# One core of Trainium2, an attention block of 2048 tokens: the order of GpSimd's instructions in the last block of queries

## The chip, the cores and the metric

The kernel runs on one core of a Trainium2 chip. The core has five engines that run their own instruction streams and meet through semaphores: TensorE (PE in the profile), VectorE (DVE), ScalarE (ACT), GpSimd (POOL) and SyncE (SP, which here only issues DMAs). DMAs are issued by SP, ACT and POOL; an issuing instruction stands in the queue of its engine like any other. The metric is the device time of one execution in microseconds. Before the change it is 1636.91 us, the median of 3 runs (1634.71 to 1638.35).

## The reference: what is computed

One layer over x of shape (1, 2048, 512): multi-head latent attention, a residual and a layer norm, then a linear layer with scale and bias, a residual and a second layer norm.

```python
cq = rms_norm(x @ w_qa.T, q_a_ln_w)              # 384 wide
q = (cq @ w_qb.T).reshape(b, s, H, 192)          # 16 heads: 128 "nope" and 64 rotary
ckv = x @ w_kva.T                                # 128 latent and 64 rotary
k_nope, v = split(rms_norm(ckv[..., :128], kv_a_ln_w) @ w_kvb.T)
scores = q_full @ k_full.T * 192 ** -0.5         # causal
out = softmax(scores) @ v                        # fp32 softmax
x = layernorm(x + out.reshape(b, s, 2048) @ w_o.T)
x = layernorm(x + x @ (weight * scale_weight[:, None]).T + bias)
```

The kernel works on latents: the key weights are folded into the queries, and the value and output weights into one product per head (wvo), so that the attention itself reads only the 128-wide latent and the rotary part.

## The kernel before, in words

**Blocks, pairs, units, heads.** The queries are cut into 4 blocks b of 512, the 16 heads into 8 pairs p, a block into 4 tiles qt of 128 queries. `units` (line 698) runs for each block over the pairs, the tiles, and (outside block 0) the two heads j of the pair. I call (b, p, qt) a unit and one head of it a half step; k = 2 qt + j counts the eight half steps of a pair. In block 3 a unit has 1664 to 2048 keys, in two tiles of up to 1024.

**A half step of block 3**, in the code's order (lines 750 to 763):

1. `settle` (line 461), where j is 0: for the units whose sums are complete, DVE adds them, takes the reciprocal and turns it (L468 to L473), and POOL writes the result to a small DRAM tensor, `rows` (16 KB, L476).
2. `prepare_output` (line 865): loads for the output, at fixed half steps, issued by POOL. In pair 6: `wv` at k = 2 (1 MB, L871). In pair 7: the first part of `wo` at k = 1 (1 MB, L862), `o` and `iv` of pairs 0 and 1 of block 0 at k = 2 and 3 (512 KB each, L823 and L839), the second part of `wo` at k = 4, `o` of pair 2 at k = 7. At k = 5 and 6 DVE and ACT multiply and split what pairs 0 and 1 brought (`latent_split`, L849, L64, L65).
3. `head_scores` (line 483): PE writes the scores into PSUM (L438, L441); DVE takes the maximum (L510) and the bias (L517, L518). In between the head before runs on: ACT copies its probabilities to fp16 (L563), POOL subtracts to get the low part (L564, two instructions), DVE transposes both (L546) and SP sends them to `ring` in the layout that the values need (L553). Then ACT takes the exponentials (L532), into `pr` tiles of which there are five.
4. `fill`: parts of the projection of the next pair, or in pair 7 of `value_output` (L198, which reads `wv` and `wo`).
5. `run_values` (line 795): half a unit of values. The first half of `values` (line 603) has POOL load `iv`, the reciprocals of the sums, from `rows` into all partitions (128 KB, L612, two buffers); PE multiplies the first keys (L619). The second half does the other keys, and DVE multiplies the result with `iv` into `ot` (L628), which SP writes to DRAM. In the steady state the first half of unit u stands in the second half step of the unit two later, and the second half in the first half step of the unit three later.

**After the last unit** (lines 930 to 957) PE accumulates the output of pairs 0 and 1 of block 0 (`accumulate`, L888). After the second accumulation of pair 0 the code finishes the last head, calls `settle`, and asks POOL for `o` of pair 3 (L823) and `iv` of pairs 2 and 3 (L839), and SP for the other two parts of `wo`. `latent_split` of pair 2 follows, then the last values, then `latent_split` of pair 3. What comes later in the code reads the rest of `o` and `iv` through SP.

**What sets the order.** The framework's planner runs a timeline of its own when the kernel is built, and from it picks the order of instructions of each engine. Inside `tc.manual_schedule(engines=...)` the engines named keep the order of the code. From block 1 on PE and SP are named (line 914). From the unit (3, 0, 1) on, DVE and ACT are named too (line 729), until the end of the last values (the ExitStack `ctx_f`). POOL is ordered by the planner throughout. So `rows`, `iv`, the loads of `prepare_output` and the subtractions L564 stand on POOL where the planner put them: the trace shows `rows` of a unit behind the two L564 of its last head, `iv` of a unit from about the time at which one of its two buffers is free, and four of the loads of pair 7 at 1280 us, while the scores of pair 6 are running.

Of the kernel before, what the change touches and what calls it, by code (L numbers as in the profile page):

```python
# [49 lines left out]
def mla_block(ctx: ExitStack, tc: tile.TileContext, a, out):  # L50
    nc = tc.nc
    ET = mybir.EngineType
# [140 lines left out]
    def value_output(p, pool, tag):  # L193

        wvo = state["wvo"][p]
        for j in range(2):
            ps = pool.tile([P, HID], F32, tag=tag, name=f"ps_wo{2 * p + j}")
            nc.tensor.matmul(ps, state["wv"][:, 2 * p + j], state["wo"][2 * p + j], start=True, stop=True)  # L198
            split(ps, wvo[:, 0, j, :], wvo[:, 1, j, :], kvln_o)
            yield  # L200
# [125 lines left out]
    def put_in(all=False):  # L326
        kept = []
        for n, dst, src in later:
            if n == 0 or all:
                nc.sync.dma_start(dst, src)  # L330
            else:
                kept.append([n - 1, dst, src])
        later[:] = kept
# [65 lines left out]
    def project_nope(b, p, direct=None):  # L399
        if direct is None and ("wq", b, p) not in state:  # L400
            load_wq(b, p)
        w = state.pop(("wq", b, p)) if direct is None else direct
        cq = state["cq"]
        qn = blk.tile([P, 2, 2, QB], F32R, tag="qn", name=f"qn{b}_{p}")
        for j in range(2):
            ps = psum["m"].tile([P, QB], F32, tag="m", name=f"ps_qn{b}_{p}_{j}")
            n = 0
            for lt in range(LT):
                for i, k in ((0, 0), (0, 1), (1, 0)):
                    nc.tensor.matmul(  # L410
                        ps, w[:, i, lt, j * P : (j + 1) * P], cq[:, k, lt, :], start=n == 0, stop=n == 8
                    )
                    n += 1
            split(ps, qn[:, 0, j, :], qn[:, 1, j, :], kvln)
            if j == 1:
                state["qn", b, p] = qn
                if b or p == NPAIR - 1:
                    load_wq(*((b, p + 1) if p + 1 < NPAIR else (b + 1, 0)))
                if p == NPAIR - 1:
                    load_block(b + 1)  # L420
            yield

    def project(b, p):
        if p % 2 == 0:
            yield from project_pe(b, p // 2)
        yield from project_nope(b, p)
# [144 lines left out]
    def pair_scores(pool, b, p, qt, nk):  # L571
        t = 4 * b + qt
        r = rq[:, t : t + 1]
        w = max(nk, 256)
        ps = psum["s"].tile([P, 2, 512], F32, tag="s", name=f"s{b}_{p}_{qt}")
        for mask in [score(ps[:, j, :], 0, w, b, p, j, qt, nk - P) for j in range(2)]:
            mask()
        neg = small.tile([P, 2], F32, tag="neg", name="neg")
        nc.vector.tensor_reduce(neg, ps[:, :, :nk], axis=AX.X, op=ALU.max, negate=True)
        bias = small.tile([P, 2], F32, tag="bias", name="bias")  # L580
        nc.vector.tensor_scalar(bias, neg, r, LOG_UP, ALU.mult, ALU.add)
        pr = pool.tile([P, 2, nk], F32, tag=f"pr{qt}", name=f"pr{b}_{p}_{qt}")
        for j in range(2):
            nc.scalar.activation(
                pr[:, j, :],
                ps[:, j, :nk],
                AF.Exp,
                bias=bias[:, j : j + 1],
                scale=r,
                accum_out=sums_of(b, p, qt, j),  # L590
            )
        return pr
# [41 lines left out]
    def fill(n=1):  # L634
        while n > 0 and fillers:
            try:
                next(fillers[0])
                n -= 1
            except StopIteration:
                fillers.pop(0)  # L640

    def drain():
        while fillers:
            fill()
# [48 lines left out]
    def flush():  # L693
        while probs:
            for _ in probs.pop():
                pass

    def units(pool, ring, b):
        lag = min(ring.shape[1] // (2048 * (b + 1)) - 1, 3) if b else 2

        for p in range(NPAIR):
            put_in(True)


            if p + 1 == NPAIR:
                at = (1, 2, 4, 5) if b < NB - 1 else (1, 3, 5, 7)
            elif p % 2 == 0 and p + 2 < NPAIR:
                at = (0, 1, 2, 3) if (b, p) == (1, 0) else (0, 1, 3, 4)
            else:
                at = (3, 4)  # L710
            if b and p % 2 == 0 and p + 2 < NPAIR:
                fillers.append(project_pe(b, p // 2 + 1))
            if p + 1 < NPAIR:
                fillers.append(project(b, p + 1) if b == 0 else project_nope(b, p + 1))
            elif b + 1 < NB:
                fillers.append(project(b + 1, 0))
            if b == NB - 1 and p == NPAIR - 1:
                ctx_p.close()
                pcr = state["pcr"] = ctx.enter_context(
                    tc.tile_pool(name="pcr", bufs=2, side="right", reuse_waits="tile")  # L720
                )
                state["wvo"] = [pcr.tile([P, 2, 2, HID], F32R, name=f"wvo{p}", bufs=1) for p in range(EARLY)]
                for i in range(EARLY):
                    fillers.append(value_output(i, psum["m"], "m"))
                at = (3, 4, 5, 6)
            for qt in range(4):
                nk = (4 * b + qt + 1) * P
                if (b, p, qt) == (NB - 1, 0, 1):
                    ctx_f.enter_context(tc.manual_schedule(engines={ET.PE, ET.SP, ET.DVE, ET.Activation}))
                if (b, p, qt) == (0, NPAIR - 1, 3):  # L730
                    s0, PT = -4 * nk, prj.tile([P, 4 * nk], F16, tag="ph", name="carry")
                elif b == 0:
                    s0, PT = -4 * nk, pool.tile([P, 4 * nk], F16, tag=f"PT{qt}", name=f"PT{p}_{qt}")
                else:
                    s0, PT = None, place(ring, 2048 * (b + 1), 4 * nk, (b, p) == (2, NPAIR - 1) and qt > 0)
                if nk <= 512:
                    pi = pair_scores(pool, b, p, qt, nk)
                    flush()
                    probs.append(pair_probs(pool, b, p, qt, nk, PT, pi))
                    if qt == 1:  # L740
                        settle((b, p))
                    fill()
                    next(side[0], None)
                    if p and qt % 2:
                        next(side[1], None)
                    if qt % 2:
                        next(side[0], None)
                    run_values(lag)
                    run_values(lag)
                else:  # L750
                    for j in range(2):
                        if 2 * qt + j == 1 if b < 2 else j == 0:
                            settle((b, p))
                        prepare_output(b, p, 2 * qt + j)
                        prev = probs.pop() if probs else iter(())
                        pi = head_scores(pool, b, p, j, qt, nk, prev)
                        probs.append(head_probs(pool, b, j, nk, PT, pi))
                        if (b, p, qt, j) == (1, 0, 1, 0):
                            half_values()
                            half_values()  # L760
                        if 2 * qt + j in at:
                            fill()
                        run_values(lag + (b == 3 and j == 0))
                if b:
                    tile_ = PT.entry
                    tile_[0] = values(b, p, qt, nk, PT)
                    vals.append(tile_)
                else:
                    vals.append([values(b, p, qt, nk, PT), 0, s0, s0 + 4 * nk])
            drain()  # L770
        if b and b < NB - 1:
            flush()
        elif b:
            next(probs[0])
# [7 lines left out]
    def place(ring, n, need, dense):  # L782

        entry = [None, 0, None, None]

        def get():
            if entry[2] is None:
                s0 = room(n, ring.shape[1], need, dense)
                entry[2:] = [s0, s0 + need]
            return ring[:, entry[2] : entry[3]]  # L790

        get.entry = entry
        return get

    def run_values(depth):

        for _ in range(1 + len(vals) - depth):
            half_values()
# [345 lines left out]
```

## Time and profile before

| what | value |
|---|---|
| runs | 1634.71, 1636.91, 1638.35 us |
| the profiled execution: its time | 1638.56 us |
| its span, first to last instruction | 1636.8 us |
| granted clock of TensorE, mean | 0.99 |
| busy: PE, DVE, ACT, POOL | 96%, 69%, 56%, 52% of the span |
| POOL's costliest group, L564 | 613.2 us in 320 instructions |
| PE's waits for the exponentials, L438 for L532 | 13.9 us in 10 waits |
| DVE's waits for POOL, L546 for L564 | 72.2 us in 81 waits |
| ACT's waits for the ring transfers, L532 | 61.1 us in 34 waits |
| an `iv` load from `rows` in block 3, issue to landing | median 5.4, longest 11.7 us |

Times in the text count from the span's start. In the profile a line such as "L564 POOL ... hlpr<-pr,hlpr" gives the line of the code, the engine, and what is written from what. In a timeline the first column is the start, the second the time from the first to the last instruction of the row, "x2" the number of instructions, and the brackets how long the engine was idle before and what ended that. Block 3 begins near 880 us; its unit (3, 0, 1), from which four engines keep the code's order, follows some 15 us later. The last scores run at about 1365, and after 1450 PE works on the output almost without a pause.

### The profile page before, as it was taken

To read this page: it belongs to the slowest core of one execution; us is meant where nothing else is said; L and a number is where in the kernel's file an instruction comes from. 1 tells how busy PE (TensorE), PEld (TensorE's weight loads), DVE (VectorE), ACT (ScalarE), POOL (GpSimd) and SP (SyncE) were. 2 spreads that over 40 slices of the span, in tenths; PEclk is the share of its full clock that TensorE was granted. 3 is DMA by queue.
4 is the path that set the end of the run, shared out by engine and by line. 5 is a ranking of instruction groups with operands and counts; after the bars stand their busy time and mean duration, and the time that the engine had idled before them with its cause. 6 is when DMAs were issued, how large, how long until landed. Compare 5 with 4: busy or idle time off the path is not lost. (4 is left out here: it accounts for less than half of the span.)

```text
span 1636.8 us, 27536 instructions
## 1 busy us (share of the span) xinstructions
PE 1575.2 (96%) x9292; PEld 1294.5 (79%) x9292; DVE 1130.0 (69%) x1874; ACT 918.3 (56%) x1529; POOL 846.0 (52%) x701
## 2 busy tenths in 40 slices
PE   9799998899999999999999999999999998999998
PEld 7688876788888888888887778888887776678876
DVE  5668665577677777777777678778677676575464
ACT  5557564666665757666665665666666654321120
POOL 2345553454554766667765566666666665011011
PEclk9899999999999999999999999999999999999999
DMA  6988676676776878787787767867777777962030
GB/s 213 265 238 267 194 203 164 175 185 172 191 206 171 217 179 202 162 206 181 199 195 180 177 153 174 184 160 160 177 156 192 211 178 210 320 197 77 32 117 33
DMA packets 259436, 297.60 MB, mean 182 GB/s; under 512 B 35264, under 2 KB 227136, under 8 KB 258272
## 3 DMA queue, kind: packets, MB, share of 16 engines
q1 hardware_dynamic: 241008, 251.63, 55.4%
q0 software_dynamic: 11376, 34.52, 12.0%
q10 hardware_dynamic: 6912, 9.70, 2.0%
q8 instruction: 74, 1.21, 0.3%
q14 instruction: 66, 0.54, 0.1%
HBM read 99.94 MB, written 36.44 MB: 83 GB/s over the span
## 5 line engine op out<-in xcount | busy, mean ns | idle before, releaser
L564 POOL TENSOR_TENSOR hlpr<-pr,hlpr 128x1024 f16<-128x1024 f32 (+3 forms) x320 | 613.2, 1935 | 327.2 <-ACT hlpr L563 297.9
L438 PE MATMUL s<-Kn,qn 128*128 128x512 f32 (+4 forms) x1920 | 510.3, 373 | 22.3 <-ACT pr L532 13.9
L532 ACT ACTIVATE pr<-s,bias,rq 128x1024 f32<-128x1024 f32 (+3 forms) x320 | 325.4, 1021 | 343.2 <-issue 178.3
L510 DVE TENSOR_REDUCE neg<-s 128x1 f32<-128x1024 f32 (+3 forms) x320 | 310.0, 985 | 133.2 <-PE s L441 75.0
L438 PEld LDWEIGHTS s<-Kn,qn 128*128 128x128 f32 x1920 | 334.3, 189 | 72.7 <-ACT pr L532 19.9
L619 PE MATMUL o<-ring,V 128*128 128x256 f16 x3024 | 373.1, 273 | 7.4 <-DMA ring<-pr 5.3
L546 DVE STREAM_TRANSPOSE pr<-hlpr 128x1024 f32<-128x1024 f32 (+7 forms) x256 | 311.5, 1223 | 97.9 <-POOL hlpr L564 72.2
L438 PE MATMUL s<-Kp,pe 128*128 128x512 f32 (+4 forms) x1280 | 362.9, 364 | 5.5 <-DMA pe<-prod 5.5
L619 PEld LDWEIGHTS <-V 128*128 128x128 f16 x3264 | 301.1, 96 | 82.7 <-issue 32.0
L563 ACT ACTIVATE hlpr<-pr 128x1024 f16<-128x1024 f32 (+3 forms) x320 | 338.2, 1113 | 4.9 <-DVE pr L546 1.0
L438 PEld LDWEIGHTS s<-Kp,pe 128*128 128x128 f32 x1280 | 233.6, 189 | 36.4 <-DMA pe<-prod 5.7
L410 PE MATMUL ps_qn<-cq,wq 128*128 128x512 f32 x576 | 150.0, 405 | 2.1 <-DMA wq<-wq_d 1.9
L989 POOL TENSOR_TENSOR lnr<-lnt,nhalf 128x1 f32<-128x1 f32 x32 | 21.3, 671 | 213.3 <-DVE lnt L988 213.2
L410 PEld LDWEIGHTS ps_qn<-cq,wq 128*128 128x128 f32 x576 | 105.5, 192 | 23.1 <-DVE xl L65 1.1
L68 DVE SCALAR_TENSOR_TENSOR qn<-ps_qn,kvln,qn 128x512 fp32r<-128x512 f32 x64 | 47.5, 744 | 45.5 <-ACT qn L67 45.2
L599 POOL TENSOR_TENSOR hl<-pr,hl 128x128 f16<-128x128 f32 (+3 forms) x64 | 56.8, 908 | 37.7 <-ACT hl L598 37.3
L372 PE MATMUL ps_pe<-cq,wpe 128*128 128x512 f32 x288 | 75.3, 407 | 0.2 <-DMA cq<-cq_d 0.2
L64 ACT ACTIVATE oh<-o 128x1024 fp32r<-128x1024 f32 x28 | 29.7, 1061 | 79.6 <-PE acc L888 49.1
L888 PE MATMUL acc<-wvo,oh 128*128 128x512 f32 x224 | 71.5, 401 | 1.0 <-ACT pr L532 0.6
L64 ACT ACTIVATE xt<-tp 128x512 fp32r<-128x512 f32 x16 | 9.6, 598 | 94.8 <-PE tp L1008 94.8
L532 ACT ACTIVATION_READ_ACCUMULATOR pr<-s,bias,rq 128x1 f32 x320 | 61.8, 193 | 0.0
L372 PEld LDWEIGHTS ps_pe<-cq,wpe 128*128 128x128 f32 x288 | 53.4, 193 | 10.6 <-issue 0.3
(458 smaller groups left out, 1777.4 us busy)
## 6 DMA issues: line engine op xcount, KB each, us to landing
ring<-pr SPq DMA_DIRECT2D x384, 128.0 KB, 2.9
wq<-wq_d SPq DMA_DIRECT2D x22, 768.0 KB, 6.7
ring<-pr SPq DMA_DIRECT2D x128, 112.0 KB, 3.4
o<-ot_d SPq DMA_DIRECT2D x28, 512.0 KB, 5.5
ot_d<-ot SPq DMA_DIRECT2D x97, 128.0 KB, 2.7
ring<-pr SPq DMA_DIRECT2D x128, 96.0 KB, 2.4
ring<-pr SPq DMA_DIRECT2D x64, 192.0 KB, 4.1
ring<-pr SPq DMA_DIRECT2D x64, 176.0 KB, 5.3
```

The lines of the kernel that those rows point to most:

```text
L68: nc.vector.scalar_tensor_tensor(l, ps, scale, h.bitcast(F32), ALU.mult, ALU.subtract)
L372: nc.tensor.matmul(ps, w[:, i, lt, x * P : (x + 1) * P], cq[:, k, lt, :], start=n == 0, stop=n == 8)
L410: nc.tensor.matmul(ps, w[:, i, lt, j * P : (j + 1) * P], cq[:, k, lt, :], start=n == 0, stop=n == 8)
L438: nc.tensor.matmul(ps[:, :w], lhs, K[:, i, c0 : c0 + w], start=n == 0, stop=n == 4 and not by_product)
L510: nc.vector.tensor_reduce(neg[:, ti : ti + 1], v, axis=AX.XY, op=ALU.max, negate=True)
L532: nc.scalar.activation(pr[:, x : x + n * w].rearrange("p (a c) -> p a c", a=n), v, AF.Exp, bias=bias, scale=r, accum_out=sums_of(b, p, qt, ...
L546: nc.vector.transpose(sq.rearrange("p (k c r) -> p k c r", k=4, r=32), words.rearrange("p (c k r) -> p k c r", k=4, r=32))
L563: nc.scalar.activation(hl[:, 0, c], pr[:, c], AF.Copy)
L564: nc.gpsimd.tensor_tensor(hl[:, 1, c], pr[:, c], hl[:, 0, c], ALU.subtract)
L599: nc.gpsimd.tensor_tensor(hl[:, j, 1, :], pr[:, j, :], hl[:, j, 0, :], ALU.subtract)
L619: nc.tensor.matmul(ps[:, :256], vt[:, i, k % 4, :], v[:, :, l, k, :], start=n == 0, stop=n == 3 * kts - 1)
L888: nc.tensor.matmul(acc, l[:, t, c], state["wvo"][p][:, i, j, :], start=p == 0 and j == 0 and n == 0, stop=p == NPAIR - 1 and j == 1 and n ...
```

## The change

POOL is added to the engines that keep the code's order from the unit (3, 0, 1) to the end of the last values. No instruction, tile or buffer is added or taken away.

```diff
                 if (b, p, qt) == (NB - 1, 0, 1):
-                    ctx_f.enter_context(tc.manual_schedule(engines={ET.PE, ET.SP, ET.DVE, ET.Activation}))
+                    ctx_f.enter_context(tc.manual_schedule(engines={ET.PE, ET.SP, ET.DVE, ET.Activation, ET.Pool}))
```

## The prediction

> **What bounds the kernel now.** I read the page's busy shares first, then who waits for whom, then the timeline of POOL (GpSimd) with the waits of PE (TensorE) beside it. The page says that PE carries the span:
>
> ```profile
> PE 1575.2 (96%) x9292; PEld 1294.5 (79%) x9292; DVE 1130.0 (69%) x1874; ACT 918.3 (56%) x1529; POOL 846.0 (52%) x701
> ```
>
> So a change on POOL, which is 52% busy, pays only where PE stands still. From 960 to 1250 us the waits of PE are empty: in pairs 1 to 5 of block 3 nothing that POOL does reaches the end. PE waits again from 1256 us. The timeline of POOL there, with each operation's start, its length and what held the engine before it in brackets, shows four places.
>
> ```profile
> 1243.31 0.56 POOL L871 DMA_DIRECT2D wv<-in_wv_dram  x1
> ...
> 1249.10 0.58 POOL L476 DMA_DIRECT2D rows(3, 5, 3)_14360<-inv(3, 5, 3)_14358  x1
> 1254.78 0.76 POOL L612 DMA_DIRECT2D iv<-rows(3, 5, 3)_14360  x1 [5.10 <-DMA rows(3, 5, 3)_14360<-inv(3, 5, 3)_14358]
> 1255.55 7.77 POOL L564 TENSOR_TENSOR hlpr<-pr,hlpr 128x1024 f16<-128x1024 f32 x4
> ...
> 1280.18 0.53 POOL L823 DMA_DIRECT2D o<-ot_d  x1
> 1280.71 0.77 POOL L839 DMA_DIRECT2D iv<-inv_d  x1
> 1281.47 0.54 POOL L823 DMA_DIRECT2D o<-ot_d  x1
> 1281.99 0.76 POOL L839 DMA_DIRECT2D iv<-inv_d  x1
> 1282.74 0.53 POOL L862 DMA_DIRECT2D wo<-in_wo_dram  x1
> 1283.29 2.40 POOL L564 TENSOR_TENSOR hlpr<-pr,hlpr 128x1024 f16<-128x1024 f32 x1
> ...
> 1302.86 0.76 POOL L612 DMA_DIRECT2D iv<-rows(3, 6, 2)_14852  x1 [2.24 <-DVE neg L510]
> 1303.64 2.40 POOL L564 TENSOR_TENSOR hlpr<-pr,hlpr 128x1024 f16<-128x1024 f32 x1
> 1305.96 0.55 POOL L862 DMA_DIRECT2D wo<-in_wo_dram  x1
> ```
>
> Five loads (3 MB) start within 3 us at 1280, in pair 6, though the code asks for them in pair 7, and an iv load sits in front of the subtractions L564 until its rows have landed (5.10 us). What PE pays, from the timeline of ACT and PE:
>
> ```profile
> 1293.16 1.10 ACT L532 ACTIVATE pr<-s,bias,rq 128x896 f32<-128x896 f32 x1 [4.86 <-DMA ring<-pr]
> 1299.35 0.97 PE L438 MATMUL s<-Kn,qn 128*128 128x512 f32 x3 [2.34 <-ACT pr L532]
> 1314.50 0.71 PE L438 MATMUL s<-Kn,qn 128*128 128x320 f32 x3 [1.63 <-ACT pr L532]
> ```
>
> **The order that comes.** The code fixes it. Of a unit (one 128-query tile qt of a pair), half step j=0 gives POOL: rows of the unit before, asked-for loads, two L564 of the head before. j=1 gives: asked-for loads, two L564, then iv of the unit two before (the first half of that unit's values stands there; its ot, which reads iv, ends the next half step). Today POOL does rows after the two L564, and iv as soon as a buffer is free. No instruction is added or removed; 31 rows, 31 iv and the output's loads move.
>
> **What goes, each by its row.**
> - iv no longer waits for rows that have just left: the 5.10 us wait at 1254.78 goes, and with it two PE waits behind it, 0.55 at 1256.52 and 1.06 at 1264.73. Gain 1.6 us.
> - The clump at 1280 goes from pair 6: the PE wait of 2.34. Gain 2.3.
> - At 1302 L564 stood behind the iv that waited 2.24, and wo0 (0.55) stood between two L564 of one head; the PE wait of 1.63 at 1314.50 came of this chain (DVE's transposes then waited 1.74 and 1.68 for L564). Gain 1.6.
> - At 939.39 an iv issue (0.79) stands between two L564 of one head and DVE waits 1.98 and 1.91 for them; PE waits 2.31 at 948.14. Gain 0.8.
> - The chain that ends last runs through POOL at 1350.54 and 1361.45, through two o issues of 0.55 and 0.49 between L564s. These loads leave that place. Gain 1.0.
>
> Sum 7.3 us.
>
> **What comes.**
> - rows ahead of L564: 0.56 us of issue, plus the wait until DVE has made inv (at 1244.44 L564 would start 1.3 later: inv ends at 1245.15). DVE's turn is late by up to as much, but iv no longer stands between L564s (0.78). In pairs 1 to 5 PE has no wait, and a score buffer is free some time before it is wanted (the exponential ended at 1062.83, the matmul began at 1064.27). I take 0; bounds 0 and 7 passages between pairs at 0.5, 3.5.
> - iv comes up to 21 us later. Its ot reads it one half step after the two L564: the L564 of 1045.83 would end 0.8 earlier, as no iv stands before it, so iv would leave at about 1047.1 and land, by the median of 5.4, at 1052.5; ot is at 1057.01. Least is to spare where a pair ends: the second L564 of (3, 3, 0)'s first head ended at 1078.10, and 5.4 later is 1083.5, with ot of (3, 2, 2) at 1083.84. 0.
> - wv leaves at about 1261 instead of 1243.31, its 1 MB into the next half steps. The 1 MB of before cost 0.55 at most (the PE wait of 1256.52 follows 3.48 of ACT's wait for ring). I take 0.5; bounds 0 and 1.1.
> - wo0, two pairs of o and iv, and wo1 (1 MB a half step) now meet the ring transfers of pair 7. From 1311 to 1348 DMA is 0.76 busy, which leaves 8.9 us of the 37; the window of 1290 to 1294 shows 384 GB/s at full share, so 4 MB ask for about 11 us more of all engines (an estimate from those rows). Below: 0, if spread loads hide behind the scores. Above: 6.2, ACT's waits for ring behind the clump (4.86 and 1.30). The nearest row is what PE paid for 3 MB at once, 2.34. I take 2.3.
> - The tail. Today the two iv of pairs 2 and 3 stand before the last rows:
>
> ```profile
> 1377.53 1.52 POOL L839 DMA_DIRECT2D iv<-inv_d  x2
> 1379.64 0.56 POOL L476 DMA_DIRECT2D rows(3, 7, 3)_15713<-inv(3, 7, 3)_15711  x1 [0.59 <-DVE inv(3, 7, 3)_15711 L473]
> 1389.23 0.75 POOL L612 DMA_DIRECT2D iv<-rows(3, 7, 3)_15713  x1 [9.04 <-DVE ot L628]
> ```
>
> ```profile
> 1383.87 1.23 DVE L849 TENSOR_TENSOR o<-o,iv 128x1024 f32<-128x1024 f32 x1 [3.89 <-DMA iv<-inv_d]
> ```
>
> In the code's order rows come first (1379.64), then the o of pair 3 (0.55; today at 1361.39), then these iv: the first leaves at 1380.8 instead of 1377.5. It landed in 6.3; POOL's iv loads have a median of 8.4, and SP's 2 MB of wo (1382.71) are now beside it. With 8.4 it lands at 1389.2, and L849 is 5.3 late. Behind L849 on DVE wait the split of its pair, the last three ot and L849 of pair 3, and for the first ot the PE values of the last unit: ot ends 5.3 later than 1387.83, PE wanted its buffer at 1391.09, so PE stops 2.0 us. The loads that follow in the chain (o, 10.26 us at 1394.93, against 3.5 to 3.7 for the same 512 KB in quiet) stand in a queue anyway, which takes up part of it; the 512 KB that now move after 1380 add 1.5 at the 341 GB/s of 1380 to 1420. I take 2.0; bounds 1.5 and 5.3.
>
> **The sum.** -7.3 + 0 + 0 + 0.5 + 2.3 + 2.0 = -2.5 us. The profiled execution took 1638.56 (span 1636.8 and 1.76 around it), so 1636.1; it is 1.65 above the median of 1636.91, so against the median **1634.4**. The rivals' times below are against the median too.
>
> A rule speaks against the change. The row: loads that left 50 us before their first use cost 2.34 of PE time and made ring late; the same engines carry both. The Trainium skill, "DMA: Bandwidth & Descriptors", section "Rules for kernel authors", says to issue a DMA early and wait for it late, so that its fixed cost is hidden. By the rule the moves could only lose: without the gains of 7.3 the sum would be +4.8, about 1641.7. The trace agrees with it in the tail alone, where DVE already waits 3.89 for a load.
>
> **Rivals.**
> 1. The spread loads hide. For it: pair 6's wv and pair 5's wq of 768 KB pass with PE waits of 0.6 or none. Against: ACT waits for ring even now (2.32 at 1334.92). wv and pair 7 cost 0, the tail 1.5: -5.8, 1631.1.
> 2. Slower: POOL's small iv land behind the bulk loads of their own queue. The row: iv(3, 6, 1) took 11.7 us behind the clump. iv(3, 6, 2) would leave at 1321.5, behind wo0 and ahead of the first o: with 11.7 it lands at 1333.2, and ot at 1327.71 is 5.5 late, on the chain. In the tail the iv takes 10.5, as SP's did: L849 7.4 late, PE 4.1. Sum -7.3 + 0.5 + 2.3 + 5.5 + 4.1 = +5.1, 1642.0. The first price begins at a landing of 6.2 us; with the tail's 4.1 the sum is above 0 from 6.6 and above 3.3 from 9.9.
> 3. The change hardly does what it says: POOL's new order only trades waits that DVE and PE absorb, as in pairs 1 to 5, and the tail takes back what pair 6 gives; 0 to -1, so -0.5: 1636.4.
>
> **Chances.** Forecast 0.34, rival 1 0.29, rival 2 0.24, rival 3 0.13. About 0.2%, 3.3 us, is what a measurement can tell from no change. Rival 1 is faster by more, and a small part (0.05) of the forecast's case, if the tail absorbs more: 0.34. The same: the rest of the forecast and rival 3: 0.42. Slower: 0.24. The range runs from rival 1's 1631.1 less 1.6 (the ring waits that POOL's earlier L564 may save) to rival 2's: 1629.5 to 1642.0. The forecast's own range is 1632.9 to 1636.5.
>
> **What would show it.** Right: no POOL wait for a rows transfer; the waits of PE at 1256, 1264 and 1299 gone; o and wo loads from about 1311 on, one to a half step; L849 of pair 2 waiting 7 to 10 us for its iv. Rival 1: PE without waits for L532 in pair 7. Rival 2: DVE's L628 waiting for iv, with landings over 9. Wrong altogether: PE waits in pairs 1 to 5, or another order of DVE, SP and ACT after 1390, which the planner makes anew, and which I count as nothing.

## The result and the profile after

The changed kernel takes **1650.14 us**, the median of 4 runs (1646.65 to 1652.67), against 1637.22 for the kernel before in the same comparison: ratio **1.0073**, 95% interval 1.0046 to 1.0099. The forecast was 1634.4 with a range to 1642.0, so the sign was wrong and the time is outside the range. The profiled execution took 1650.30 (span 1648.2, mean granted clock 0.986). The line of busy times of the changed kernel, as the page has it:

```profile
PE 1578.0 (96%) x9292; PEld 1296.5 (79%) x9292; DVE 1133.8 (69%) x1874; ACT 917.8 (56%) x1529; POOL 845.9 (51%) x701
```

The work is the same; what came is waiting. To see where, I took from the trace the start of the mask matmul L441, with which the scores of a head end, for each head of block 3, and compared it with the same head of the profile before. The difference grows or shrinks by stretch (us, negative is gained; the last column is the change of the span). A stretch ends with the second head of the next pair's first unit, so "pairs 0 to 5" ends with the unit (3, 6, 0), and "pair 6" with (3, 7, 0), where PE's wait at 1314.50 stood before; "tail" is what follows the last mask matmul:

| execution | up to (3, 0, 0) | pairs 0 to 5 | pair 6 | pair 7 | tail | span |
|---|---|---|---|---|---|---|
| after | +4.0 | +4.4 | -7.0 | +4.6 | +5.4 | +11.4 |

Up to (3, 0, 0) the order is the same in both kernels; those 4.0 us are not the change's (experiment 6). The rest has four places.

**Start of pair 0.** POOL's timeline, then DVE's:

```profile
896.63 0.56 POOL L476 DMA_DIRECT2D rows(3, 0, 0)_10572<-inv(3, 0, 0)_10570  x1 [3.75 <-DVE inv(3, 0, 0)_10570 L473]
897.21 3.91 POOL L564 TENSOR_TENSOR hlpr<-pr,hlpr 128x1024 f16<-128x1024 f32 x2
```

```profile
897.34 4.87 DVE L65 TENSOR_TENSOR prod<-prod,ph 128x1024 fp32r<-128x1024 f32 x1 [1.00 <-ACT ph L64]
```

POOL stands 3.75 us at `rows`, so L564 starts only at 897.21, and DVE's L65, which follows 0.13 later, takes 4.87 us. In the profile before it took 1.39:

```profile
895.38 1.39 DVE L65 TENSOR_TENSOR prod<-prod,ph 128x1024 fp32r<-128x1024 f32 x1 [1.00 <-ACT ph L64]
```

The exponentials come late and PE waits 1.87 at 906.15.

**Passages between pairs**, POOL at the passage from pair 2 to pair 3:

```profile
1070.27 0.78 POOL L612 DMA_DIRECT2D iv<-rows(3, 2, 1)_12066  x1
1072.41 0.54 POOL L476 DMA_DIRECT2D rows(3, 2, 3)_12386<-inv(3, 2, 3)_12384  x1 [1.36 <-DVE inv(3, 2, 3)_12384 L473]
1072.96 4.75 POOL L564 TENSOR_TENSOR hlpr<-pr,hlpr 128x1024 f16<-128x1024 f32 x2
```

Here, and at the passage from pair 4 to 5, L564 starts 1.9 us later than it could: a wait of 1.36 for DVE, and the issue. PE, which the prediction saw without a wait in these pairs, now has them. Its waits from 960 to 1290 us (columns: total, number, longest), after and then before, where both stand in pair 6:

```profile
PE s L438 <- ACT pr L532: 3.9, 5, 1.0
```

```profile
PE s L438 <- ACT pr L532: 1.6, 2, 1.1
```

**Pair 6** gains, as forecast: the waits of PE at 1256, 1264, 1299 and 1314 are gone. **Pair 7** has the loads, where the code asks for them:

```profile
1315.87 0.55 POOL L862 DMA_DIRECT2D wo<-in_wo_dram  x1
...
1327.39 0.53 POOL L823 DMA_DIRECT2D o<-ot_d  x1
1327.91 0.76 POOL L839 DMA_DIRECT2D iv<-inv_d  x1
...
1332.53 0.55 POOL L823 DMA_DIRECT2D o<-ot_d  x1
1333.08 0.77 POOL L839 DMA_DIRECT2D iv<-inv_d  x1
...
1344.43 0.55 POOL L862 DMA_DIRECT2D wo<-in_wo_dram  x1
```

The median ring transfer of 128 KB takes 5.1 us there instead of 2.8, ACT waits for ring 3.65 at 1324.91 and 2.98 at 1340.63, and PE 1.11 at 1330.42 and 2.04 at 1343.12. The small `iv` land in 5.1 to 5.5 us: rival 2's mechanism did not come about in this pair.

**The tail**, POOL, DVE and PE:

```profile
1385.67 0.56 POOL L476 DMA_DIRECT2D rows(3, 7, 3)_15713<-inv(3, 7, 3)_15711  x1 [2.06 <-DVE inv(3, 7, 3)_15711 L473]
...
1386.76 1.51 POOL L839 DMA_DIRECT2D iv<-inv_d  x2
...
1399.14 0.75 POOL L612 DMA_DIRECT2D iv<-rows(3, 7, 3)_15713  x1 [9.85 <-DVE ot L628]
```

```profile
1394.87 1.23 DVE L849 TENSOR_TENSOR o<-o,iv 128x1024 f32<-128x1024 f32 x1 [8.86 <-DMA iv<-inv_d]
...
1415.92 0.42 DVE L628 TENSOR_TENSOR ot<-o,iv 128x256 f32<-128x256 f32 x1 [9.06 <-DMA ot_d<-ot]
```

```profile
1416.40 3.78 PE L207 MATMUL ps_wo<-wo,wv 128*128 128x512 f32 x4 [8.20 <-DVE ot L628]
```

Read upward from PE: it stands 8.20 us, until DVE has written the last `ot`. In the profile before the same wait is 0.92:

```profile
1402.02 1.98 PE L207 MATMUL ps_wo<-wo,wv 128*128 128x512 f32 x4 [0.92 <-DVE ot L628]
```

What did the last `ot` wait for? Not for the last `iv`, which left POOL at 1399.14 and landed 8.6 us later. The bracket of its row names `ot_d<-ot`: `ot` has two buffers, and the one that it needs is held until SP has written the `ot` of (3, 7, 1) to DRAM. SP's timeline there, after and then before (L823 is a load of `o`, L330 the write):

```profile
1398.52 4.55 SPq L823 DMA_DIRECT2D o<-ot_d  x1
1403.18 2.00 SPq L330 DMA_DIRECT2D ot_d<-ot  x2
```

```profile
1387.55 1.40 SPq L823 DMA_DIRECT2D o<-ot_d  x1
1389.05 1.74 SPq L330 DMA_DIRECT2D ot_d<-ot  x2
```

The first of these writes lands 12.6 us after its issue, 12.4 in the profile before. In all 18 traces of this document the last `ot` starts 0.12 or 0.13 us after that landing, and 2.5 to 9.1 us after the last `iv` has landed. So the chain runs: L849 waits 8.86 for an `iv` that left behind `rows`; the `ot` of (3, 7, 1), which stands behind L849 on DVE, ends 5.0 us late (1398.83 against 1387.83, less the 6.0 that the kernel was late by then); SP's issue of `o` ahead of the write takes 4.55 instead of 1.40, so the write leaves 8.1 late; and the last `ot` is 8.4 late. Why that issue took longer isn't shown.

And the same four matmuls take 3.78 us where before they took 1.98. The table of windows says why (columns: stretch, PE busy, granted clock, DMA share, GB/s):

```profile
1411.00:1412.00 1.00, 0.00 (x0) 0.88 0.94 373
1412.00:1413.00 1.00, 0.00 (x0) 0.50 0.67 248
...
1416.00:1417.00 1.00, 0.60 (x1) 0.50 0.28 111
...
1421.00:1422.00 1.00, 1.00 (x4) 0.50 1.02 406
1422.00:1423.00 1.00, 1.00 (x5) 1.00 1.01 401
```

From 3.6 us after PE stopped (1408.20) until 1422 the granted clock is 0.50. PE works 5.6 us in that time and loses half of it, 2.8, on top of the 8.2 that it stood. In the profile before, the clock from 1380 to 1440 is 1.00 throughout.

### The profile page after: what moved, and what is told of

It reads as the page before. It is cut to its first block, busy times and chain, and to the rows that moved or that the text cites. A ratio compares the mean times of both kernels' runs of the same rounds, so it can differ in the third digit from the quotient of the medians.

```text
span 1648.2 us, 27529 instructions
## 1 busy us (share of the span) xinstructions
PE 1578.0 (96%) x9292; PEld 1296.5 (79%) x9292; DVE 1133.8 (69%) x1874; ACT 917.8 (56%) x1529; POOL 845.9 (51%) x701
## 4 chain that ended last, share of the span: by engine, by line
PE 60%; DMA 14%; issue 7%; DVE 6%; POOL 6%; SPq 4%; ACT 3%; ACTq 0%; POOLq 0%; DVEq 0%
PE s L438 24%; PE o L619 13%; PE acc L888 9%; PE ps_qn L410 5%; DMA ring<-pr 5%; POOL hlpr L564 5%; SPq L553 4%; PE ps_pe L372 2%; PE ff L1022 2%; DVE pr L546 2%; DMA wq<-wq_d 2%; DMA ot_d<-ot 1%; DMA pe<-prod 1%; DMA PT<-pr 1%; PE ps_cq L271 1%
## 5 line engine op out<-in xcount | busy, mean ns | idle before, releaser
L564 POOL TENSOR_TENSOR hlpr<-pr,hlpr 128x1024 f16<-128x1024 f32 (+3 forms) x320 | 611.5, 1931 | 312.4 <-ACT hlpr L563 303.4
L438 PE MATMUL s<-Kn,qn 128*128 128x512 f32 (+4 forms) x1920 | 512.0, 374 | 20.2 <-ACT pr L532 12.6
```

The costliest lines, as they stand in the source:

```text
L438: nc.tensor.matmul(ps[:, :w], lhs, K[:, i, c0 : c0 + w], start=n == 0, stop=n == 4 and not by_product)
L564: nc.gpsimd.tensor_tensor(hl[:, 1, c], pr[:, c], hl[:, 0, c], ALU.subtract)
```

## The experiments

My theory when I planned the experiments, from the two traces: three prices (rows ahead of L564; the moved loads in pair 7; the late `iv` in the tail), each raised by the clock that falls after a stall of PE, against pair 6's gain. The rival: the prediction's covers hold, and the differences are what one execution differs from another. Every time below is against the kernel before on the same chip in the same comparison; the stretches are those of the table above, against the one profile of before that the prediction read.

| kernel | time, us | ratio, 95% interval | up to (3, 0, 0) | pairs 0 to 5 | pair 6 | pair 7 | tail |
|---|---|---|---|---|---|---|---|
| before_again | 1636.96 | 0.9975, 0.9957 to 0.9994 | +8.2 | -1.5 | -2.3 | +1.5 | -1.0 |
| pool_p0_5 | 1654.12 | 1.0080, 1.0057 to 1.0103 | +6.2 | +4.0 | +9.0 | -0.8 | +2.9 |
| pool_p6 | 1640.25 | 0.9992, 0.9977 to 1.0007 | +4.1 | -4.9 | -2.1 | -0.3 | -0.1 |
| pool_p7 | 1642.01 | 1.0012, 0.9996 to 1.0028 | +2.9 | -2.5 | -5.6 | +5.0 | +1.0 |
| pool_tail | 1646.20 | 1.0035, 1.0015 to 1.0054 | +4.3 | -2.7 | -0.7 | +1.7 | +4.4 |
| after_again | 1649.41 | 1.0074, 1.0053 to 1.0095 | +4.9 | +2.8 | -7.0 | +5.6 | +4.9 |
| rows_behind | 1645.08 | 1.0044, 1.0026 to 1.0062 | +0.5 | -1.7 | -6.2 | +6.7 | +3.5 |
| tail_first | 1647.30 | 1.0051, 1.0031 to 1.0071 | +0.6 | +2.3 | -7.0 | +4.0 | +1.2 |
| all_behind | 1637.66 | 1.0000, 0.9988 to 1.0013 | +7.1 | -2.4 | -7.0 | +1.6 | -1.1 |
| loads_behind | 1648.57 | 1.0053, 1.0033 to 1.0073 | +6.4 | +3.3 | -7.0 | +5.1 | +3.3 |
| from_pair_6 | 1637.92 | 0.9988, 0.9972 to 1.0004 | +2.9 | -3.6 | -7.0 | +5.1 | -0.5 |
| no_wo | 1646.82 | 1.0050, 1.0028 to 1.0072 | +7.1 | +2.9 | -7.0 | +1.5 | +4.5 |
| after_spread | 1644.83 | 1.0047, 1.0031 to 1.0062 | +3.7 | +3.4 | -7.0 | +2.6 | +3.6 |
| spread | 1638.84 | 0.9997, 0.9977 to 1.0016 | +2.6 | -3.0 | -7.0 | +1.7 | +4.4 |
| spread_124567 | 1638.58 | 0.9990, 0.9970 to 1.0009 | +5.4 | -1.9 | -7.0 | +0.7 | +2.7 |
| spread_023567 | 1640.86 | 1.0006, 0.9989 to 1.0023 | +4.5 | +1.4 | -7.0 | +5.4 | +2.2 |

### 1. One part of the change alone: pool_p0_5, pool_p6, pool_p7, pool_tail

POOL keeps the code's order in one stretch only, by a stack of its own that is opened and closed there (shown for pair 6):

```diff
+            if (b, p) == (NB - 1, 7):
+                ctx_o.close()
+            if (b, p) == (NB - 1, 6):
+                ctx_o.enter_context(tc.manual_schedule(engines={ET.Pool}))
             for qt in range(4):
```

In the first three PE, DVE, ACT and SP have exactly the order of before. In pool_tail the planner, as in after, also moves the values of the last unit on PE behind two accumulations.

> POOL in the program's order only from (3, 0, 1) to the end of pair 5; before and after that POOL is planned as in the kernel before, and the other engines' orders are those of before. Theory A (the 4.4 us that the trace of after loses between pair 0 and pair 5 come from rows standing ahead of L564, at the passages between pairs): 1641 to 1642, 4 to 5 us over before, with PE waits at the starts of the odd pairs. Theory B (the prediction: these moves are hidden, and the 4.4 us are what one execution differs from another): 1637, within 1.5 us of before.

> POOL in the program's order in pair 6 alone; pair 7's loads can't start before pair 7. Theory A (the gains that I forecast are real, and reach the end): 1630 to 1632, 5 to 7 us under before (the trace of after gains 7.0 there; the prediction had 5.5 to 6.3 for its terms in pair 6, less 0.5 for wv). Theory B (the gain is taken back behind, since the loads now meet the transfers of pair 7 under either order): 1635 to 1637.

> POOL in the program's order in pair 7 alone, the tail planned; loads of pair 7 leave in pair 7, one to a half step. Theory A (the loads collide with ring, and a PE stall of about 2 us halves the granted clock for some 3 us): over before by 2 to 5 us, with the clump's 2.3 in pair 6 saved and 4.6 lost in pair 7 (as the trace of after shows); 1639 to 1642. Theory B (the prediction's terms: -2.3 for the clump, -1.0 for the o issues, +2.3 for the loads): 1636.

> POOL in the program's order only from the tail on (rows ahead of the loads of pairs 2 and 3); everything ahead of it as before. Theory A (the late load of inv_d of pair 2 makes DVE's L849 and the ot of the last units late, PE stalls over 5 us at L207, and the granted clock of TensorE falls to a half for about 10 us): 5 to 12 us over before, 1642 to 1649. Theory B (the prediction: 2.0, at most 5.3): 1639. If L207 stalls and the clock stays at 1.00, the clock's part of theory A is wrong.

pool_p0_5 costs 13 us, more than theory A gave: +4.0 in its own pairs, and +9.0 in pair 6, which is the boundary's doing: where the planner takes over it issues two late `iv`, `wv` and `rows` at once (1252.18 to 1254.30), and PE waits 4.19 at 1267.94. pool_p6 was a poor test, since my expectation was wrong about the kernel: the planner still put the five loads of pair 7 into pair 6 (1276.02 to 1278.61), and only 2.1 were gained. With pool_p7 they do leave: pair 6 gains 5.6 though its own order is the planner's, and pair 7 loses 5.0. So most of the gain of pair 6 is that the loads go, and in this execution pair 7 pays for it: theory A, and a tie in time. pool_tail has theory A's tail (+4.4, a PE wait of 8.54 at L207, the clock at 0.50 for 10 us).

### 2. The changed kernel again: after_again

> The changed kernel once more, on the chip of the next three, so that these have a number to stand against. Ratio to before as in the first runs, 1.005 to 1.010: 8 to 16 us over. What its trace loses from head to head in block 3 should repeat (2 us at the start of pair 0, 2 at the passage to pair 3, 2 at the passage to pair 5, 7 gained in pair 6, 4.6 lost in pair 7, 5 in the tail); what doesn't repeat was chance.

It repeats: the ratio, pair 6 to 0.1 us, the same waits at the same places. Only the 4.4 of pairs 0 to 5 (now 2.8) differs by more than 1 us.

### 3. rows behind L564: rows_behind

```diff
-                nc.gpsimd.dma_start(rows.rearrange("g t q -> (g t) q"), inv)
+                if key[0] == NB - 1:
+                    rows_due.append((rows, inv))
+                else:
+                    nc.gpsimd.dma_start(rows.rearrange("g t q -> (g t) q"), inv)
...
                         pi = head_scores(pool, b, p, j, qt, nk, prev)
+                        send_rows()
```

`send_rows` issues what is in `rows_due`; in the tail it stands right behind `settle`.

> As after, but in block 3 each rows leaves behind the two L564 of its half step. All else on POOL stays in the program's order. Theory A (POOL stands at rows until DVE has made inv, and L564 behind it starts late: 5.7 us in pairs 0 to 5 and 1 to 3 of the 4.6 in pair 7): 6 to 9 us under after, the losses at the start of pair 0 and at the passages to pairs 3 and 5 gone. Theory B (the prediction's cover holds, and what after loses in these pairs comes from iv being late, or from chance): within 2 us of after.

Pairs 0 to 5 go from +4.4 and +2.8 to -1.7, where kernels with before's order stand too: theory A there. DVE's L65 at the start of pair 0, and POOL at the passage to pair 3, in rows_behind (its lines are shifted: L574 is the subtraction, L466 `rows`):

```profile
896.99 1.23 DVE L65 TENSOR_TENSOR prod<-prod,ph 128x1024 fp32r<-128x1024 f32 x1 [1.00 <-ACT ph L64]
```

```profile
1064.19 4.75 POOL L574 TENSOR_TENSOR hlpr<-pr,hlpr 128x1024 f16<-128x1024 f32 x2
1068.85 0.57 POOL L466 DMA_DIRECT2D rows(3, 2, 3)_12386<-inv(3, 2, 3)_12384  x1
```

At the passage `rows` no longer waits; at the start of pair 0 it waits 0.96, but behind L564. No wait of POOL's own making stands ahead of L564, and L65 takes 1.23. `iv` is as late as in after, so that is acquitted. Pair 7 did not improve (+6.7). Its loads stand closer together there: the first `o` leaves 5.6 us behind the first `wo`, 11.5 in after, where POOL waits 3.79 at `rows` ahead of it; whether that makes the difference to after's 4.6 and 5.6 isn't shown. By the medians the kernel is 4.3 under after, less than the 6 to 9 expected, since only pairs 0 to 5 gained; the two intervals overlap.

### 4. The tail's loads first: tail_first

```diff
-                        settle()
                         ctx_l.close()
...
                         for i in range(2):
                             latent_rows(0, EARLY + i, nc.gpsimd.dma_start)
+                        settle()
```

and `o` of pair 3 is asked for at k = 7. PE, DVE, ACT and SP then have before's order.

> As after, but the o of pair 3 leaves with the o of pair 2 in the last half step, and in the tail the two iv of pairs 2 and 3 leave ahead of the last rows, as in before; PE, DVE, ACT and SP then have before's order again. Theory A (the late iv of pair 2 makes the tail's loss): 4 to 6 us under after, L207's PE wait back to about 1 us, granted clock 1.00 from 1400 to 1430. Theory B (the tail is late because SP's loads of wo share the engines with these, in whichever order): within 2 us of after.

The tail loses 1.2 instead of 5.4 and 4.9, and the clock from 1380 to 1440 is 1.00. DVE's and PE's lines of tail_first:

```profile
1386.33 1.23 DVE L849 TENSOR_TENSOR o<-o,iv 128x1024 f32<-128x1024 f32 x1 [3.84 <-DMA iv<-inv_d]
```

```profile
1405.77 1.98 PE L207 MATMUL ps_wo<-wo,wv 128*128 128x512 f32 x4 [0.88 <-DVE ot L628]
```

Theory A by the trace: L849 waits 3.84 and no longer 8.86. By the medians the kernel is only 2.1 under after, and the two intervals overlap. What this run can't tell is how much of it is PE's order, which went back as well.

### 5. All POOL's issues behind L564, and the loads alone: all_behind, loads_behind

all_behind has the edits of 3 and 4, and the loads of `prepare_output` stand behind `head_scores`, while its splits stay ahead (`split_output`); loads_behind has that last edit alone.

```diff
-                        prepare_output(b, p, 2 * qt + j)
+                        split_output(b, p, 2 * qt + j)
...
                         pi = head_scores(pool, b, p, j, qt, nk, prev)
+                        prepare_output(b, p, 2 * qt + j)
```

> As after with both edits, and in pair 7 the loads of a half step too leave behind its two L564. Theory A (what after loses is order on POOL: the waits ahead of L564 and the tail): 11 to 15 us under after, that is 0 to 4 us under before, since the gain of 7 in pair 6 stays. Theory B (the 4 MB that move to pair 7 cost what after loses there, 4.6, wherever they stand in their half step): 2 to 5 us less than that, at or over before.

> As after, but in pair 7 the loads of a half step leave behind its two L564; rows stay ahead of L564, and the tail is that of after. Theory A (in pair 7 it is the place of the loads, ahead of L564 and of the ring transfers that follow on it, that costs; with the rows moved alone the pair lost 6.7, with both moved 1.6): pair 7 loses 1 to 3 us instead of 4.6 to 5.6, so 2 to 4 us under after. Theory B (both have to stand behind L564, since L564 waits at whichever is ahead): within 1 us of after.

all_behind takes back all of the change's loss: 11.8 us under after, no different from before. So the loss lies in where POOL has `rows`, the loads of pair 7 and the loads of the tail. PE's order in the tail is that of before again too, so POOL's own part there isn't separated. loads_behind is theory B by the trace, with pair 7 at +5.1; by the time it lies 8.6 over before, where after lies 11.8 and 12.9 over, which would be theory A, but the intervals overlap. That pair 7 needs both edits, as all_behind's +1.6 seemed to say, fell with from_pair_6 (7), which has all_behind's order on POOL and PE from pair 6 on and lost 5.1. So two executions of one order differ by 3.5 us in pair 7; 1.7 of it is one more window of half the clock (1331.98 and 1359.29 in from_pair_6, 1352.85 in all_behind). The place within a half step isn't shown to matter.

### 6. The kernel before again: before_again

> The kernel before, unchanged, as a second profiled execution. If the profiled execution that I read was a typical one, this trace stands within 1 us of it at every head of block 3. If not (three experiments with the same order there ran the same way), it loses about 4 us against it before block 3, and gains 2.5 to 5 on it between (3, 0, 1) and (3, 1, 0), where the execution that I read has PE's wait of 2.31 at 948.14; then the gain of 0.8 that I counted for the iv issue at 939.39 was no gain of the change's. Ratio 1.000, within 0.0015.

The stretches are as expected: the execution that I read was the fastest of 18 up to block 3, by 4.4 us on the mean of the others, and slower than its peers right after. The kernel against itself gave 0.9975, outside of 0.0015 either way and with an interval that excludes 1: **differences of 4 us in these comparisons are not to be trusted.** That bears on rows_behind, tail_first and loads_behind, whose differences from after are of that size; all_behind's 11.8 is well above it.

### 7. Keeping only the gain: from_pair_6

As all_behind, but POOL is planned until pair 6 begins.

```diff
+            if (b, p) == (NB - 1, 6):
+                ctx_f.enter_context(tc.manual_schedule(engines={ET.Pool}))
```

> POOL planned up to the end of pair 5, as in before; from pair 6 on in the program's order, with rows and loads behind L564 and the tail's iv ahead of the last rows. Theory A (what is left of the change when its three costs are taken out is pair 6's gain of 7, of which pair 7 takes back 1 to 2): 4 to 6 us under before, 1632 to 1634. Theory B (the gain in pair 6 is only borrowed: the loads that left there must be paid for in pair 7 or the tail, so all_behind's tie with before is all there is): within 2 us of before.

Theory B: pair 7 took back 5.1 of 7.0, and the ratio 0.9988 can't be told from 1. The tail shows that an early `iv` is not all that its end needs: L849 waits only 3.96, and still PE stands 3.48 at L207, since the write of the `ot` of (3, 7, 1) lands 16.3 us after that `ot` (13.6 in before, 13.1 in all_behind, 17.0 in after).

### 8. What pair 7 pays for: no_wo, after_spread, spread, spread_124567, spread_023567

```diff
             if k == 1:
-                load_wo(0, blk, "qn")
+                w = state["wv"].rearrange("p (a b) c -> p a (b c)", b=4)
+                state["wo"] = [w[:, j] for j in range(4)] * 2
...
-            if k == 4:
-                load_wo(1, state["pcr"], "wo")
```

This is no_wo, made of after: the two loads of `wo` are left out, and the matmuls that need them read `wv`. The other four only change the k at which loads leave: after_spread is after with loads at 1, 2, 4 and 6; spread is from_pair_6 with the same; the last two are from_pair_6 with the half steps in their names.

> As after, but the two loads of wo in pair 7 (2 of the 4 MB there) are left out, and the matmuls that use them read wv in their place; so the output isn't the reference's. Theory A (the bytes meet the ring transfers): pair 7 loses 0 to 2 us instead of 4.0 to 5.6, so 3 to 5 under after. Theory B (order on POOL, or work that stands in pair 7 in any case): pair 7 loses 4 to 6 as before, and the time is that of after within 1 us. Pairs 0 to 5 (about 3 us from the start of pair 0 on by the trace) and the tail (4 to 5) as in after under both.

> As after, but o and iv of pair 1 leave in half step 4 instead of 3, and the second wo in half step 6 instead of 4, so that the 4 MB stand in half steps 1, 2, 4 and 6 and not in 1 to 4. Theory A (bytes per half step are what counts): pair 7 loses 1 to 3 instead of 4.0 to 5.6, 2 to 4 under after; the tail may take back 0 to 2, as the second wo lands 20 us later. Theory B: pair 7 loses 4 to 6, the time is after's.

> POOL planned to the end of pair 5, from pair 6 on in the program's order, rows and loads behind L564, the tail's iv ahead of rows, and the loads of pair 7 in half steps 1, 2, 4 and 6. Theory A: pair 6 gains 7, pair 7 takes back 1 to 3, the rest as in before: 4 to 6 us under before, about 1633. Theory B (pair 7 takes back 5 wherever the loads stand): 2 us under before, which the comparison can't tell from no change.

> As spread, but the second wo leaves in half step 5 and the o of pair 2 in half step 6 (loads in half steps 1, 2, 4, 5, 6 and 7 of pair 7). Theory A (bytes per half step decide, and the tail is paid for by late loads alone): pair 6 gains 7, pair 7 takes back 1 to 3, the tail 0 to 1: 3 to 6 us under before. Theory B (what isn't paid in pair 7 is paid in the tail): pair 7 and the tail together take back 5 to 6, the time is before's within 2 us.

> As spread, with the loads of pair 7 in half steps 0, 2, 3, 5, 6 and 7; the first wo leaves half a step earlier than the code of before asks for it. Theory A: as for the run before, 3 to 6 us under before; if the first wo meets the ring transfers of the last unit of pair 6, pair 6 gains 5 to 6 instead of 7. Theory B: before's time within 2 us.

Without the 2 MB pair 7 loses 1.5, which two executions of before's order lose too (1.5, 1.7); spread out, it loses 2.6, 1.7 and 0.7. That points to theory A, the bytes and their density, but doesn't show it: all_behind and from_pair_6 differ by as much in one order, and spread_023567 goes against it (+5.4, with the first `wo` half a step early; pair 6's gain stayed at 7.0, so the condition that I had set was not it). Nor do the traces say how the bytes would act. ACT's waits for ring in pair 7 add up to 1.4 to 3.2 us in the five executions whose loads leave in pair 6, and to 4.3 to 9.2 in those with loads in pair 7, but among these they don't follow the loss: 4.5 where spread_023567 loses 5.4, 5.9 where spread_124567 loses 0.7. The median ring transfer doesn't either (5.1 in no_wo as in after). In the tails of the three spread kernels made of from_pair_6, PE stands 4.4 to 5.6 at L207 with an early `iv`; there too the write of the `ot` of (3, 7, 1) lands late, 16.3 to 18.1 us after it.

In time, no_wo is only about 4 us under after by the ratios, with overlapping intervals, and the three kernels made of from_pair_6 are within 2 us of before, which is their theory B. The net gain: of the 7.0 us of pair 6, pair 7 and the tail take back 3.3 in the best case (0.7 and 2.7), 6.1 in spread, and no kernel is told from before. The idea of the change is worth less than these comparisons resolve.

## Why the prediction was wrong, step by step

Means over the executions that share an order in a stretch give each term its size, freed of the one profile of before, whose start was lucky and whose pairs 0 and 1 were not. For pairs 0 to 5 the seven are after, after_again, pool_p0_5, tail_first, loads_behind, no_wo and after_spread; the nine are the others but rows_behind and all_behind.

| step | forecast | measured | from |
|---|---|---|---|
| rows ahead of L564, iv late (pairs 0 to 5) | 0, at most 3.5, less a gain of 0.8 | +5.4 | code's order +3.3 (7 executions), before's order -2.1 (9) |
| pair 6 with wv | -5.0 | -6.0 | code's order -7.0; before, before_again, pool_tail -1.0 |
| pair 7: loads less the o issues | +1.3 | +3.7 | after, after_again, tail_first, loads_behind +4.8; the same three +1.1 |
| tail | +2.0, at most 5.3 | +4.6 | 7 executions with rows first +4.2; before, before_again, pool_p6 -0.4 (+3.7 with the tails of pool_p0_5 and pool_p7, +2.9 and +1.0, where these loads stand as in before too) |
| sum | -2.5 | +7.7 | measured by the medians: 11.8 and 12.9 |

The rest of 4 to 5 us (5 to 6 with the smaller tail) isn't assigned; the intervals of the two comparisons reach down to 7.5 and 8.7.

- **rows ahead of L564: this step failed most.** I named the mechanism and its seven passages, and covered it with a score buffer that was free 1.4 us before it was wanted. That was one place. At the start of pair 0 and at the passages to pairs 3 and 5 there is less, and there it cost 1.5 to 2 us each. I had priced the wait of POOL, and not what the shifted L564 then collides with at the start of pair 0: DVE's L65. Part of the price there is the clock: three of the seven executions in the code's order lose 3.0 to 3.2 against the profile before, and the clock falls in these three alone; the other four lose 1.4 to 1.5. At the two passages no L65 runs beside L564, and the way from L564 to PE there isn't followed; that `rows` is the cause rests on rows_behind, which loses 0.6 and 0.2 there, the kernels with before's order 0.1 in the mean. My sentence "wrong altogether: PE waits in pairs 1 to 5" came true.
- **iv up to 21 us later: right, 0.** rows_behind keeps it and loses nothing in pairs 0 to 5.
- **The iv issue between two L564 at 939.39: no gain.** Seven of the eight other executions with before's order there pass that place 3.1 to 4.7 us faster. The wait of 2.31 at 948.14 that I counted belonged to that execution, and the clock fell behind it (0.50 for 3.4 us from 949.6), which I did not look at.
- **Pair 6: right,** in sign, place and nearly in size. pool_p7 shows that it is the clump of loads that matters most.
- **Pair 7: the collision that I forecast fits the sign, the size was too small; the mechanism isn't shown (experiment 8).** I took what PE paid for 3 MB at once, 2.34. The 3.7 measured lies between that and the upper bound, 6.2, and single executions of orders with these loads in pair 7 run from +0.7 to +6.7. The 1.0 for the o issues can't be seen.
- **The tail: the first link was right, the last one missed.** L849 was forecast 5.3 late; it was 5.0 (1394.87 less 1383.87, less the 6.0 that the kernel was late by then). But I followed it to the first ot, where PE would stop 2.0. The stop came at the last, and through an engine that I did not follow: late L849, late `ot` of (3, 7, 1), late write of it by SP, its buffer held, late last `ot`, and 8.2 us of PE. I had written that the planner's new order after 1390 counts as nothing; it too came, and its part isn't separated.
- **The clock: a term that I had not at all.** See below; 2.8 us in the tail and 1.7 at 906 and at 1343 in the profiled execution.

Of the rivals, the slower one had the right sign, but not the mechanism: its late `iv` in pair 7 did not come about, `rows` was not in it, and its tail, 4.1, is near the measured 3.7 to 4.6 by luck, since it too ends at the first `ot`.

## What to carry to other kernels

An issue that waits holds all that stands behind it on its engine, so before a queue is put in the code's order ask of every waiting entry what is ready behind it; a DMA that needs another engine's result belongs behind the work that doesn't. A chain through a small ring of buffers is followed to the last user of the ring, not the first, and on through the engine that empties the buffers: here two `ot` buffers and SP's write. And one profile is one draw: a wait is a term of the sum only if a second execution has it, and a stall of PE near 2 us is priced with the clock that may fall after it.

## What the runs showed of the hardware

**The clock falls after short stalls.** In the 18 traces, from 880 to 1480 us, PE has 119 waits of 0.7 to 1.7 us, and the granted clock stays at 1.00 after every one. Of 47 waits of 1.7 to 2.45 us, 25 are followed by a clock of 0.50, and all 14 longer ones are. It lasts one or more windows of 3.4 us: each costs 1.71 us where PE works through it. Two like stalls of 2 us thus cost 2 or 3.7 us, and which of the two can't be told ahead from these traces. The Trainium skill, "TensorE: Matmul & The Clock Gate", section "What's actually happening", has the clock fall to half after an idle window of about 3.4 us, with windows that run freely. The length of the windows agrees; as a threshold for one stall the measurement decides, and 1.8 us sufficed (1.76 at 1310.48 in pool_p6).

**DVE and POOL get in each other's way.** L65 on DVE took 4.87 us in after when it began 0.13 us after POOL's two L564, and ended 1.1 after them; with L564 moved it took 1.23. The Trainium skill, "SBUF — State Buffer", section "Who interferes with whom", says that a DVE instruction with two inputs in SBUF contends with a GpSimd instruction that reads SBUF, and that the order of issue decides which of two is held. This row agrees for the first L564; the second began at 899.55, 2.2 us after L65, and went ahead of it too.
